# Rows and columns of a DRAM array change places: a stage of its own against element-wise DMAs inside the scans

## The chip, the cores and the metric

The kernel runs as one program on one core of a Trainium2 chip. The metric is device time in microseconds of one execution; the time of the kernel before is the median of 3 runs.

## What is computed

The input is one image of 256 x 256 positions with 128 channels. Two layers work on it, each on a group-normalized copy, and each adds its result to the image. The first is row-wise attention with a bias that comes from the pairs. The second is a selective scan over the image in four directions, and the change lies in it:

```python
x_flat = xc.reshape(b, d, L)                                    # rows, one after the other
x_t    = jnp.transpose(xc, (0, 1, 3, 2)).reshape(b, d, L)       # columns, one after the other
xs     = concat([x_flat, x_t, flip(x_flat), flip(x_t)], axis=1) # k = 0, 1, 2, 3
x_dbl  = einsum('bkdl,kcd->bkcl', xs, x_proj_w)
dts, Bs, Cs = split(x_dbl, [8, 24], axis=2)                     # rate input, B, C
delta  = softplus(einsum('bkrl,kdr->bkdl', dts, dt_w) + dt_b)
h      = exp(delta_t * A) * h + (delta_t * x_t) * B_t           # 65536 steps, 16 states, 256 channels
y      = einsum('bkdn,bkn->bkd', h, C_t)
```

Scans 0 and 2 read the image in row order (2 from the end), scans 1 and 3 in column order (3 from the end). The four results are summed in image order, normalized, gated and projected.

## The kernel before

All data is f32. `build` runs the stages one after the other: `group_stats`, `pair_norm`, `attention`, `conv`, `swap`, `scans`, `output`. What passes between them lies in DRAM (`SCRATCH`): among it `xk`, the scans' input by token, `bk`, B of the four scans, `y`, the sum so far, and the rate input and C of the scans, 24 rows (8 and 16) of 65536 tokens for each scan. `conv` works on 8 image rows at a time and ends each with stores that ACT issues: `mid_dc<-dc` twice (lines 579 and 580), `mid_xk<-xk` (577), `mid_y<-y` (578) and four `mid_bk<-bk` (582). `dc0` has the 48 rows of scans 0 and 2, `dc1` those of scans 1 and 3. Both have their tokens in row order.

Scans 1 and 3 want their 48 rows in column order. `swap` (lines 585 to 612) makes that array, `dcT`, from `dc1`. In two halves, it loads 96 partitions of 128 x 128 elements into the tile `a` (16 DMAs of SP, pieces of 512 bytes), copies them with the two axes exchanged into `o` on ACT and DVE by turns (lines 606 and 608), and stores them (32 DMAs of ACT, line 610).

`scans` takes the scans in the order k = 0, 2, 1, 3. Each has 64 blocks of 1024 tokens. In each scan the first 4 and the last 6 blocks are written out, and the 54 between run in a hardware loop of 3 passes with 18 blocks each, whose DRAM addresses come from registers. The order of the instructions on every engine is written by hand (`tc.manual_schedule()`), in 32 steps a block, one for each state m and half h of the channels:

- `recur`: DVE runs the recurrence along the 1024 tokens (`hs`, line 858, TENSOR_TENSOR_SCAN); after the second half POOL multiplies `hs` with C, which `fetch` brought (`cc<-mid_dc` or `cc<-mid_dcT`, line 826, one row of C broadcast to 128 partitions, ring of 4).
- `turn`: PE brings the input term of the next step to PSUM (`mm`, lines 846 and 848), in rings of two.
- `collect`: PE turns `hs` three states back and sums it over the states (line 617).
- `decay`: ACT computes `da` = exp(delta A) (line 839) four steps ahead, in a ring of six.
- `scale`: ACT scales with B (`dg` and `but`, lines 833 and 835) six steps ahead.
- `advance` runs the preparation of the next block as a list of pieces, each due at a step. The ones that matter here are `size` in steps 6 and 8 (`e<-mm`, line 759, ACT, after PE's `rate`, line 750), `exp` in step 9, `log` in step 10, and `one_plus` and `rest` in steps 11 and 12.

SP issues all loads and stores of the scans: `dt` (line 724, step 21 of the block two before), `bt` and `xk` (step 0 of the block before), `yb` (step 16), the store of `y` (step 8 of the block after) and a `cc` for every second step. ACT issues none in the scans. Every DMA takes one of eight completion semaphores by turns and waits until the last DMA on that semaphore has ended. The recording layer also makes a DMA wait for an earlier one that writes the same array, if it can't see that the places are distinct.

Of the kernel before, what the change touches and what calls it, by code (L numbers as in the profile page):

```python
# [28 lines left out]
F32 = mybir.dt.float32  # L29
# [6 lines left out]
P = 128  # L36
N = 256
# [7 lines left out]
KD = 4  # L45
RC = DR + DS
# [16 lines left out]
def load_consts(tc, pool, io):  # L63
    nc = tc.nc
    c = Consts()
    c.ident = pool.tile([P, P], F32, name="ident")
    nc.sync.dma_start(out=c.ident, in_=io["c_ident"])
    c.group = pool.tile([P, P], F32, name="group")
    nc.sync.dma_start(out=c.group, in_=io["c_group"])
    c.eps = pool.tile([P, 1], F32, name="eps")  # L70
    nc.vector.memset(c.eps, EPS)
    c.gn1 = pool.tile([P, 2], F32, name="gn1")
    c.gn2 = pool.tile([P, 2], F32, name="gn2")
    return c
# [507 lines left out]
                nc.scalar.dma_start(out=io["bk"][k, toks, :].rearrange("(j p) n -> p j n", p=P), in_=bk[:, k])  # L582


def swap(tc, io, src, dst):

    nc = tc.nc
    B = 128
    Q = 16
    PR = KD // 2 * RC  # L590
    s = io[src].rearrange("p (i h w) -> i p h w", h=B, w=N)
    d = io[dst].rearrange("p (w i h) -> i p w h", i=N // B, h=B)
    with tc.tile_pool(name=f"s_{dst}", bufs=1) as sb:
        for j in range(N // B):
            a = sb.tile([P, B, B], F32, name="a")
            for i in range(N // B):
                for q in range(0, B, B // 4):
                    nc.sync.dma_start(
                        out=a[i * PR : (i + 1) * PR, q : q + B // 4, :],
                        in_=s[i, :, q : q + B // 4, j * B : (j + 1) * B],  # L600
                    )
            o = sb.tile([P, B, B], F32, name="o")
            for n, q in enumerate(range(0, B, Q)):
                to, of = o[0 : N // B * PR, q : q + Q, :], a[0 : N // B * PR, :, q : q + Q].rearrange("p h w -> p w h")
                if n % 2:
                    nc.scalar.copy(to, of)
                else:
                    nc.vector.tensor_copy(to, of)
                for i in range(N // B):
                    nc.scalar.dma_start(  # L610
                        out=d[i, :, j * B + q : j * B + q + Q, :], in_=o[i * PR : (i + 1) * PR, q : q + Q, :]
                    )


def turned(nc, c, out, in_, start, stop):

    nc.tensor.matmul(out, in_, c.ident, is_transpose=True, start=start, stop=stop, skip_group_check=True)  # L617


def scans(tc, io, c):  # L620
# [11 lines left out]
    nc = tc.nc  # L632
    TB = 1024
# [6 lines left out]
    with tc.tile_pool(name="e_w", bufs=1) as wp, tc.tile_pool(name="e_1", bufs=1) as sb1, tc.tile_pool(  # L640
        name="e_2", bufs=2
# [43 lines left out]
        class Block:  # L685
# [44 lines left out]
            def advance(self, now, after):  # L730
                if self.pieces is None:
                    self.pieces = begin(self)
                while self.pieces and self.pieces[0][:2] <= (now, after):
                    _, _, f, *args = self.pieces.pop(0)
                    f(*args)

        def begin(B):

# [86 lines left out]
        def fetch(B, m):  # L825
            nc.sync.dma_start(out=ccs[m % 4], in_=B.S.C[m : m + 1, B.where()].partition_broadcast(P))
# [26 lines left out]
        def recur(B, m, h):  # L853
            hs = hss[(B.n * DS + m) % HS]
            o, d0, d1 = hs[:, h, :], das[((B.n * DS + m) * NH + h) % DA], d1s.pop(0)
            if B.S.back:
                o, d0, d1 = o[:, ::-1], d0[:, ::-1], d1[:, ::-1]
            nc.vector.tensor_tensor_scan(o, d0, d1, state[:, m, h : h + 1], ALU.mult, ALU.add)  # L858
            if h == NH - 1:

                last = 0 if B.S.back else TB - 1
                last = hs[:, :, last : last + 1]
                nc.vector.tensor_reduce(state[:, m, :], last, AX.X, ALU.max)  # L863
                for x in range(NH):
                    nc.gpsimd.tensor_tensor(hs[:, x, :], hs[:, x, :], ccs[m % 4], ALU.mult)  # L865
# [16 lines left out]
        def collect_some(most):  # L882

            for x in list(waiting):
                if most == 0:
                    break
                B, _, _, j = x
                if B.slot(j) // PB in B.free:
                    waiting.remove(x)
                    collect(*x)  # L890
                    most -= 1

        def evict(B, after, part):

            n = NJ // PB // 2
            for g in range(part * n, (part + 1) * n):
                to = B.y[:, g * PB : (g + 1) * PB, :]
                nc.vector.tensor_tensor(to, to, pys[g], ALU.add)
                if after:
                    after.free.add(g)  # L900
            if part == 1:
                nc.sync.dma_start(out=B.rows(io["y"]), in_=B.as_rows(B.y))
# [5 lines left out]
        def body(blocks, before, after):  # L908

            own = len(blocks)  # L910
            at_hand = dict(enumerate(blocks + after))
            if before:
                at_hand[-1] = before
                before.free = before.started = set(range(NJ // PB))
                d1s[:] = [mms[count[0] % 2]]

            def at(u):
                x, s = divmod(u, U)
                return (at_hand[x], *divmod(s, NH)) if x in at_hand else None

            def do(f, u):
                if at(u):
                    f(*at(u))

            if before is None:
                blocks[0].load()
                blocks[0].load_tokens()
                blocks[0].advance(U, True)
                blocks[0].free = set(range(NJ // PB))
                blocks[1].load()  # L930
                for m in range(4):
                    fetch(blocks[0], m)
                for u in range(3 * NH):
                    do(scale, u)
                for u in range(4):
                    do(decay, u)
                do(turn, 0)
            for x, B in enumerate(blocks):
                nxt = at_hand.get(x + 1)
                for s in range(U):  # L940
                    u = x * U + s
                    m, h = divmod(s, NH)
                    if s == 0 and nxt:
                        nxt.load_tokens()
                    if s == 21 and x + 2 in at_hand:
                        at_hand[x + 2].load()
                    if s == 16:
                        nc.sync.dma_start(out=B.as_rows(B.y), in_=B.rows(io["y"]))
                    if nxt:
                        nxt.advance(s, False)  # L950
                    recur(B, m, h)
                    do(turn, u + 1)
                    if at(u - LAG * NH):
                        waiting.extend((*at(u - LAG * NH), j) for j in range(NJ))
                    collect_some(len(waiting) if s == LAG * NH - 1 else share.get(s, 10))
                    if x - 1 in at_hand and s in (6, 8):
                        evict(at_hand[x - 1], B, (s - 6) // 2)
                    if nxt:
                        nxt.advance(s, True)
                    do(decay, u + 4)  # L960
                    if u == 0:
                        nc.scalar.preload_act_table_set("natural_log_exp_and_others")
                    do(scale, u + 3 * NH)
                    if h == NH - 1 and at(u + 1 + 3 * NH):
                        fetch(*at(u + 1 + 3 * NH)[:2])
            if not after:
                waiting.extend((*at(u), j) for u in range(own * U - LAG * NH, own * U) for j in range(NJ))
                collect_some(len(waiting))
                for part in range(2):
                    evict(blocks[-1], None, part)  # L970
            assert not waiting


        n = NT // TB
# [103 lines left out]
@with_exitstack  # L1078
def build(ctx: ExitStack, tc: tile.TileContext, io):
    const = ctx.enter_context(tc.tile_pool(name="const", bufs=1))  # L1080
    c = load_consts(tc, const, io)
    group_stats(tc, io, c)
    pair_norm(tc, io, c)
    attention(tc, io, c)
    conv(tc, io, c)
    swap(tc, io, "dc1", "dcT")
    scans(tc, io, c)
    output(tc, io, c)

# [44 lines left out]
```

## Time and profile before

| what | value |
|---|---|
| median of 3 runs | 28440.62 us (28439.84 to 28441.89) |
| profiled execution, span | 28447.5 us |
| PE busy | 26610.1 us (94%) |
| ACT busy | 25332.4 us (89%) |
| DVE busy | 24922.2 us (88%) |
| POOL busy | 22944.4 us (81%) |
| DMA packets | 1923996, 3630.07 MB |
| queue q1 (issued by SP) | 1424722 packets, 3339.77 MB, 34.6% of 16 engines |
| queue q10 (issued by ACT) | 496640 packets, 255.88 MB, 3.2% of 16 engines |
| DVE hs L858 | 8192 instructions, 2340 ns each |
| POOL hs L865 | 8192 instructions, 2380 ns each |
| ACT da L839 | 8192 instructions, 1139 ns each |
| ACT o L606 and DVE o L608 in swap | 8 each, median 3642 and 1906 ns |
| ACTq L610, stores of swap | 32, median 1231 ns to issue, from 4626.5 us to 4731.9 us |

The profiled execution has no time of its own beside its span; the span is 6.9 us longer than the median of the runs. In the profile, `ACTq` and `SPq` are instructions of ACT's and SP's sequencers, here the issues of DMAs, which are not counted as busy time. `L` and a number is a line of the kernel. "ACT e L759 <- PE mm L750" is a wait of ACT at line 759 that PE's line 750 ended.

### The profile page before, as it was taken

Reading aid. Unit: us, or ns where it says so; the run is one execution under the profiler, and the core shown is the slowest. Engines: PE = TensorE matmul, PEld = TensorE weight load, DVE = VectorE, ACT = ScalarE, POOL = GpSimd, SP = SyncE. Lnnn points to the kernel's source line nnn. Section 1 sums busy time; section 2 is a strip of 40 time slices with the busy share of each in tenths; the row PEclk is TensorE's granted clock in tenths of the full one; section 3 lists DMA queues with packets and bytes.
Section 4 is the critical chain, followed back from the end, with each engine's and each line's share of the span. In section 5 each row is a group of like instructions: output and inputs, shape, how many; then the busy total and the mean of one; then the engine's idle time right before and its main releaser. Section 6 shows DMA issues by size and latency. Waiting matters only on the chain. (4 is left out here: it accounts for less than half of the span.)

```text
span 28447.5 us, 528099 instructions
## 1 busy us (share of the span) xinstructions
PE 26610.1 (94%) x196490; PEld 22529.2 (79%) x196490; DVE 24922.2 (88%) x24253; ACT 25332.4 (89%) x49673; POOL 22944.4 (81%) x10118
## 2 busy tenths in 40 slices
PE   8999996999999999999999999999999999999998
PEld 3555444888888888888888888888888888888884
DVE  4777665999999999999999999999999999999987
ACT  6875224999999999999999999999999999999987
POOL 2443002999999999999999999999999999999983
PEclk9999998999999999999999999999999999999999
DMA  5112345433433333333334333333333333333335
GB/s 206 55 50 71 111 116 115 132 132 129 133 130 133 132 131 132 132 131 132 128 132 133 131 133 132 131 132 129 132 132 130 133 132 129 132 130 132 133 132 172
DMA packets 1923996, 3630.07 MB, mean 128 GB/s; under 512 B 532297, under 2 KB 1240009, under 8 KB 1889490
## 3 DMA queue, kind: packets, MB, share of 16 engines
q1 hardware_dynamic: 1424722, 3339.77, 34.6%
q10 hardware_dynamic: 496640, 255.88, 3.2%
q8 instruction: 1568, 25.69, 0.4%
q14 instruction: 1066, 8.73, 0.1%
HBM read 3002.42 MB, written 592.84 MB: 126 GB/s over the span
## 5 line engine op out<-in xcount | busy, mean ns | idle before, releaser
L865 POOL TENSOR_TENSOR hs<-hs,cc 128x1024 f32<-128x1024 f32 x8192 | 19202.5, 2380 | 1346.1 <-DVE state L863 679.9
L858 DVE TENSOR_TENSOR_SCAN hs<-da,state,mm 128x1024 f32<-128x1024 f32 x8192 | 18976.6, 2340 | 1465.4 <-PE mm L848 1074.7
L846 PE MATMUL mm<-dg,dxt 128*128 128x128 f32 x65536 | 9305.0, 287 | 1065.1 <-DVE hs L858 886.1
L846 PEld LDWEIGHTS mm<-dg,dxt 128*128 128x128 f32 x65536 | 8328.4, 199 | 2257.9 <-DVE hs L858 1897.8
L839 ACT ACTIVATE da<-delta,A 128x1024 f32<-128x1024 f32 x8192 | 9328.4, 1139 | 112.2 <-PEq L984 76.0
L617 PE MATMUL y<-ident,hs 128*128 128x128 f32 x65536 | 8511.4, 275 | 1.4 <-POOL hs L865 1.4
L835 ACT ACTIVATE but<-dxt,bt 128x256 f32<-128x256 f32 x16384 | 8150.2, 497 | 11.4 <-DVE dxt L794 11.4
L617 PEld LDWEIGHTS y<-ident,hs 128*128 128x128 f32 x65536 | 7494.1, 143 | 1.9 <-POOL hs L865 1.9
L833 ACT ACTIVATE dg<-ident,bt 128x128 f32<-128x128 f32 x16384 | 6393.1, 390 | 0.2
L848 PE MATMUL mm<-ident,but 128*128 128x128 f32 x32768 | 5092.5, 280 | 0.0
L848 PEld LDWEIGHTS mm<-ident,but 128*128 128x128 f32 x32768 | 4011.4, 146 | 0.0
L750 PE MATMUL mm<-dt,dtw 9*128 9x512 f32 x4096 | 2033.0, 615 | 265.9 <-DMA bt<-mid_bk 184.5
L385 POOL TENSOR_TENSOR an<-ex,rs 128x1024 f32<-128x1024 f32 x512 | 970.2, 1895 | 1024.5 <-PE tp L394 566.3
L780 POOL TENSOR_TENSOR lw<-lw,e 128x1024 f32<-128x1024 f32 x512 | 1207.7, 2384 | 336.3 <-ACT lw L766 336.3
L750 PEld LDWEIGHTS mm<-dt,dtw 9*128 9x128 f32 x4096 | 680.7, 184 | 959.5 <-issue 733.3
L500 POOL MEMSET pad<- 128x10 f32 x32 | 3.7, 117 | 1650.0 <-PE ps L537 1639.9
L777 POOL TENSOR_TENSOR lw<-lw,w 128x1024 f32<-128x1024 f32 x512 | 1202.9, 2375 | 0.0
L537 PE MATMUL ps<-pad,w 128*128 128x512 f32 x2048 | 954.8, 610 | 161.0 <-ACT xi L525 161.0
L372 ACT ACTIVATE ex<-sc,nm 128x256 f32<-128x256 f32 x2048 | 1013.7, 499 | 0.4
L759 ACT ACTIVATE e<-mm 128x1024 f32<-128x1024 f32 x512 | 524.7, 1025 | 522.1 <-PE mm L750 521.9
L355 DVE CUSTOM_DVE_ANT_0 sc<-ps,bias 128x256 f32<-128x256 f32 x2048 | 746.2, 421 | 117.3 <-PE ps L340 117.3
L394 PEld LDWEIGHTS tp<-ident,an 128*128 128x128 f32 x4096 | 467.5, 141 | 470.7 <-POOL an L385 235.1
(137 smaller groups left out, 18522.4 us busy)
## 6 DMA issues: line engine op xcount, KB each, us to landing
cc<-mid_dc SPq DMA_DIRECT2D x2048, 512.0 KB
cc<-mid_dcT SPq DMA_DIRECT2D x2048, 512.0 KB
xk<-mid_xk SPq DMA_DIRECT2D x256, 1024.0 KB
yb<-mid_y SPq DMA_DIRECT2D x256, 1024.0 KB
mid_y<-yb SPq DMA_DIRECT2D x256, 1024.0 KB
xt<-mid_xT SPq DMA_DIRECT2D x64, 1024.0 KB
mid_xk<-xk ACTq DMA_DIRECT2D x32, 2048.0 KB
mid_y<-y ACTq DMA_DIRECT2D x32, 2048.0 KB
```

Of the source, the lines that this page charges most:

```text
L372: nc.scalar.activation(exs[u][:, x, :], scs[u][:, e, jt, :], AF.Exp, scale=-1.0, bias=nms[u][:, e, jt : jt + 1], accum_out=sms[u][:, x : x ...
L617: nc.tensor.matmul(out, in_, c.ident, is_transpose=True, start=start, stop=stop, skip_group_check=True)
L750: nc.tensor.matmul(pu[:, q : q + T], dtw[0 : DR + 1, k, h * P : (h + 1) * P], B.dt[0 : DR + 1, q : q + T], start=True, stop=True,)
L777: nc.gpsimd.tensor_tensor(B.lw[:, h, :], B.lw[:, h, :], B.w[:, h, :], ALU.add)
L780: nc.gpsimd.tensor_tensor(B.lw[:, h, :], B.lw[:, h, :], B.e[:, h, :], ALU.add)
L833: nc.scalar.activation(dg[:, j, :], c.ident, AF.Copy, scale=B.bt[:, B.slot(j), m : m + 1])
L835: nc.scalar.activation(bu[:, j, :], B.dxt[:, DJ + j, :], AF.Copy, scale=B.bt[:, at, m : m + 1])
L839: nc.scalar.activation(da, B.delta[:, h, :], AF.Exp, scale=A[:, B.S.k * NH + h, m : m + 1])
L846: nc.tensor.matmul(d1[:, j * P : (j + 1) * P], B.dxt[:, j, hc], dg[:, j, :], start=True, stop=True)
L848: nc.tensor.transpose(d1[:, j * P : (j + 1) * P], bu[:, j - DJ, hc], c.ident)
L858: nc.vector.tensor_tensor_scan(o, d0, d1, state[:, m, h : h + 1], ALU.mult, ALU.add)
L865: nc.gpsimd.tensor_tensor(hs[:, x, :], hs[:, x, :], ccs[m % 4], ALU.mult)
```

## The change

The function `swap(tc, io, src, dst)` and its call go. In `scans` a nested function of the same name takes its place: for a block B of scan 0 (B.S.x = 0) or 2 (B.S.x = 1) it takes 24 rows of `dc1`, those of scan 1 or 3, and moves four image columns of them to where they lie in column order in `dcT`. There is one DMA for each column, issued by ACT, from DRAM to DRAM: it reads 24 x 256 elements that lie 1 KB apart, and writes them as 24 runs of 256 neighbours. Over the 64 blocks of the two scans all 256 columns of all 48 rows are moved. It is issued in step 10, after `exp` and `decay` and `scale` of step 9, and before `log`.

```diff
-def swap(tc, io, src, dst):
-    nc = tc.nc
-    B = 128
-    Q = 16
-    PR = KD // 2 * RC
-    s = io[src].rearrange("p (i h w) -> i p h w", h=B, w=N)
-    d = io[dst].rearrange("p (w i h) -> i p w h", i=N // B, h=B)
-    with tc.tile_pool(name=f"s_{dst}", bufs=1) as sb:
-        for j in range(N // B):
-            a = sb.tile([P, B, B], F32, name="a")
-            ...
@@ in scans
+        def swap(B):
+            G = KD // 2
+            rows = slice(B.S.x * RC * KD // 2 // G, (B.S.x + 1) * RC * KD // 2 // G)
+            W = TB // N
+            of = io["dc1"][rows].rearrange("p (h w) -> p h w", w=N)[:, :, B.where(N)]
+            to = io["dcT"][rows, B.where()].rearrange("p (w h) -> p w h", h=N)
+            with nc.allow_non_contiguous_dma(reason="rows and columns change places"):
+                for w in range(W):
+                    nc.scalar.dma_start(out=to[:, w, :].unsqueeze(2), in_=of[:, :, w : w + 1])
@@ in body, for each step s of a block
                     if s == 0 and nxt:
                         nxt.load_tokens()
+                    if s == 10 and not B.S.across:
+                        swap(B)
                     if s == 21 and x + 2 in at_hand:
                         at_hand[x + 2].load()
@@ in build
     conv(tc, io, c)
-    swap(tc, io, "dc1", "dcT")
     scans(tc, io, c)
```

More of the change, by code (lines that the diff above doesn't have):

```diff
@@ L582, in conv @@
                 nc.scalar.dma_start(out=io["bk"][k, toks, :].rearrange("(j p) n -> p j n", p=P), in_=bk[:, k])
-def swap(tc, io, src, dst):
-    nc = tc.nc
-    B = 128
-    Q = 16
-    PR = KD // 2 * RC
-    s = io[src].rearrange("p (i h w) -> i p h w", h=B, w=N)
-    d = io[dst].rearrange("p (w i h) -> i p w h", i=N // B, h=B)
-    with tc.tile_pool(name=f"s_{dst}", bufs=1) as sb:
-        for j in range(N // B):
-            a = sb.tile([P, B, B], F32, name="a")
[L596 to L612, printed above, removed]
 def turned(nc, c, out, in_, start, stop):
```

## The prediction

> **What bounds it now.** I read the page first (shares of the engines, their course over the span), then one scan block, the waits in the scans, and the timeline of the stage that goes.
>
> ```profile
> PE 26610.1 (94%) x196490; PEld 22529.2 (79%) x196490; DVE 24922.2 (88%) x24253; ACT 25332.4 (89%) x49673; POOL 22944.4 (81%) x10118
> ...
> ACT  6875224999999999999999999999999999999987
> ```
>
> PE leads the totals, but they mix stages. From the eighth slice on, the scans, ACT is full. The cc loads of the first two scans run from 4755.7 to 16208.7 us: 11,453 us for 128 blocks, 89.5 us each. A stretch of about one block (columns: length; busy PE, PEld, DVE, ACT, POOL; granted clock, DMA share, GB/s):
>
> ```profile
> 10000.00:10089.00 89.00, 85.70 (x675) 78.49 (x673) 82.79 (x57) 86.99 (x167) 84.01 (x37) 0.96 0.40 132
> ```
>
> ACT has the most work, 87.0 us, and in the waits from 10000 to 12000 us (22 blocks) it waits in one place only, 40.3 us in all, about 2 us a block, before the step e:
>
> ```profile
> PEld mm L846 <- DVE hs L858: 168.0, 156, 1.6
> ...
> ACT e L759 <- PE mm L750: 40.3, 43, 2.4
> ```
>
> So ACT's order of instructions sets the length of a block. Whatever holds ACT for more than 2 us a block is paid in full, since ACT can't make it up.
>
> **What is removed.** In SP's timeline the stage reaches from its first load to the first load of the scans:
>
> ```profile
> 4578.09 113.12 SPq L598 DMA_DIRECT2D a<-mid_dc  x16
> 4737.14 0.30 SPq L644 DMA_DIRECT2D dtw<-in_dt_wT  x1
> ```
>
> Nothing else is at work meanwhile, and what comes next (dt, bt and xk of scan 0) needs only what conv wrote. The whole 159 us goes.
>
> **What is added.** In each of the 128 blocks of scans 0 and 2 ACT issues four DMAs, between exp and log of step 10. Each has 24 x 256 = 6,144 elements of 4 bytes, none next to its neighbour in the source, so 6,144 descriptors (24,576 a block, 3.1 million in all; the profile counts 1.9 million packets now). None uses SBUF, and SP's queue issues nothing of it.
>
> *Engines.* In the trace's DMA records the dtw load of 8 rows ends in 8 four-byte completion writes, transfers of 48 and 128 rows in 16. A transfer of 24 rows does not divide by 16; I take 12, the largest divisor below it: 512 descriptors an engine. (Bound: 16 engines, 384 each.)
>
> *Time of a descriptor.* The trace has no element-wise transfer from DRAM to DRAM. The nearest rows, as windows:
>
> ```profile
> 2595.05:2596.05 1.00, 1.00 (x4) 0.49 (x3) 0.59 (x1) 0.73 (x2) 0.00 (x0) 1.00 0.86 6
> 4573.00:4576.00 3.00, 0.00 (x0) 0.00 (x0) 0.00 (x0) 0.00 (x0) 0.00 (x0) 0.50 0.82 86
> 4578.00:4737.00 159.00, 0.00 (x0) 0.00 (x0) 14.68 (x8) 29.23 (x8) 0.00 (x0) 0.50 1.01 158
> ```
>
> The first is the load of cw, 4-byte reads from DRAM: 1,663 records in 1 us over 16 engines, 9.6 ns per descriptor and engine. The second is the end of conv's bk stores, 64-byte writes to DRAM: 11.8 ns. The third has the loads of a, 512 bytes read at a pitch of 1 KB: at worst 433 in 2 us, 74 ns, with the data itself in it and only 48 partitions to write. I take 11.8 ns, the row that writes small pieces to DRAM. If an engine read and wrote in turn it would be 9.6 + 11.8 = 21.4 ns; upper end 74 ns. A rule speaks against the change: the Trainium skill, "DMA: Bandwidth & Descriptors", section "Specifications", says that transfers under 512 bytes are done as read-modify-write. The 64-byte row shows no price of that; no row has a 4-byte write to DRAM. If the rule bites there, the sum is that of the second rival below.
>
> *Does ACT go on after issuing?* Its timeline at the end of conv says no:
>
> ```profile
> 4557.93 0.40 ACTq L577 DMA_DIRECT2D mid_xk<-xk  x1
> 4559.19 1.50 ACTq L578 DMA_DIRECT2D mid_y<-y  x1
> 4560.73 14.45 ACTq L582 DMA_DIRECT2D mid_bk<-bk  x4
> ```
>
> The first 2,048 descriptors are accepted in 0.40 us, later ones only as earlier ones drain: when the fourth bk issue ends, 12,288 have been issued and 9,166 started, 3,122 still waiting, about 200 an engine. ACT stands meanwhile; "ACT xi L525" waits 549.1 us in 31 blocks for it, 17.7 us each. The same page's section "Issuing engines are not separate DMA queues" calls the sequencer's time to start a DMA usually small relative to the DMA; this row has it at the size of the DMA, and by the rule the sum would be that of the first rival below.
>
> *Waits.* In the built program the 54 blocks of each scan's loop, whose addresses are in registers, have every swap DMA wait for the completion of the one before. The 10 blocks outside the loop have no such wait. ACT's own queue stands behind it: log, the next da, dg and but, for which PE's turn and DVE's scan wait, and POOL's product after them. da is 4 units ahead and a unit is 89.5 / 32 = 2.8 us, so the others run on some 11 us and then stand as well.
>
> *Sum for one block.* From issue to first packet 0.86 us (L610, 4702.72 to 4703.58), from last packet to the waiter 0.80 us (4736.65 to 4737.45, DVE's memset of dt), data 512 x 11.8 ns = 6.04 us: 7.7 us for a waited DMA. In the loop: three of them, 23.1 us, and of the fourth 0.86 + 312 x 11.8 ns = 4.5 us until its last 200 fit: 27.6 us. Outside it: 0.86 + (2,048 - 200) x 11.8 ns = 22.7 us. In the first 11 us two cc fetches share the engines, 8 packets each of 159 ns: 2.5 us. The 2 us that ACT waits for e now I don't credit: in the stretch without PE work above the granted clock was 0.50, and PE at half speed after each stall will hold up e and turn about as long. That is 30.1 and 25.2 us.
>
> 108 x 30.1 = 3,251 and 20 x 25.2 = 504, together 3,755; less 159 is +3,596 us. The profiled span is 28,447.5 us, 6.9 above the median, and the page shows no time outside it, so the difference goes on the median: 28,440.6 + 3,596 = 32,040 us.
>
> Ends: 16 engines, 9.6 ns, no cc, 2 us credited: 3 x 5.35 + 0.86 + 184 x 9.6 ns = 18.7 us in the loop, 13.7 outside; 108 x 16.7 + 20 x 11.7 - 159 = +1,875, 30,320 us. 21.4 ns: 48.1 and 42.9 us, +5,870, 34,310 us. 74 ns: 3 x 39.5 + 24 + 2.5 = 145 and 140 us, +18,300, 46,700 us.
>
> Beside this: the 16 DMA engines have 0.40 of 89 us = 36 us of work a block; 12 get 24 us more, within a block of 119 us, so they are no bound. SP's DMAs share completion semaphores with the new ones; a cc fetch is issued 6 units, 17 us, ahead, and POOL stands through the stall, so I put it at nothing; uncovered, it would cost a landing of about 2 us a block, +0.26 ms.
>
> **Rivals.**
> 1. *Hidden, faster.* ACT's issues return at once as those of xk did (0.40 us), and the chain of waits is met in the 2 us of slack; then only the stage goes: 28,440.6 - 159 = 28,280 us. It decides where ACT is held below 159 / 128 + 2 = 3.2 us a block. For it: DMA share 0.40, the result is needed a scan later. Against it: bk's issues, with a quarter as many descriptors an engine, and the waits. One waited transfer alone is past 3.2 us.
> 2. *Slow elements.* 4-byte writes into the same piece of DRAM, or reads at a pitch of 1 KB, go at over 21.4 ns. At 36 ns: (0.86 + 18.4 + 0.80) x 3 + 0.86 + 11.2 + 2.5 = 74.9 and 69.9 us, +9,320, 37,760 us; at 74 ns 46,700 us. For it: the slow loads of a, and no row with such a write. Against it: those loads also moved 128 times the bytes.
> 3. *The exchange moves, but ACT isn't held in the loop beyond the ring* (waits met early): 22.7 us everywhere, 128 x 22.7 - 159 = +2,750, 31,190 us; inside my band.
>
> **How the numbers follow.** Forecast with rival 3 inside (9.6 to 21.4 ns; 30,320 to 34,310 us) 0.72; rival 2 0.23; rival 1 0.04; no measurable difference, where both would cancel, 0.01. The range takes in the band and rival 2 up to 36 ns: 30,320 to 37,760 us; beyond lie about 0.15 above and 0.05 below. Faster than 0.2% (57 us, about what a measurement of this kernel can tell) 0.04, same 0.01, slower 0.95.
>
> **What would show it.** Right: no stage between conv and scans; four swap DMA issues a block on ACT, the first three each some 8 us apart in the loop, the fourth's row about 4 us long; blocks of scans 0 and 2 near 119 us, of 1 and 3 still 89.5; q10 with 3.1 million 4-byte packets more; DVE waiting for da once a block. Wrong: blocks of 89 us, issues of under 1 us with log following at once, a swap transfer far from 6 us, or cc fetches as the longest wait.

## The result: twice the time

The changed kernel takes 57,527 us (median of 4 runs, 57,387 to 57,614), against 28,441 us. The ratio is 2.022, with a 95% interval of 2.019 to 2.025. The direction was forecast; the size was not: 29,086 us were added where 3,600 were predicted, and the time lies far above the range (37,760 us). Of the spread of cases, it is rival 2, slow elements, and beyond its dearest figure (46,700 us).

The page of the changed kernel, the lines that answer to those of before (the last is from its part 3):

```profile
PE 27689.3 (48%) x196490; PEld 23421.5 (41%) x196490; DVE 24997.0 (43%) x24245; ACT 25401.4 (44%) x49665; POOL 22879.0 (40%) x10118
...
ACT  7623232222222222332222222222223699999998
...
DMA  3147875666788888888878887666588633333334
...
q10 hardware_dynamic: 3623424, 255.90, 32.7%
```

The engines do the same work as before in twice the span. In the first two scans, now slices 4 to 31 of 40, ACT is busy in two or three tenths, while the DMA engines go up to eight tenths. The last two scans look as before. ACT's queue q10 has 3.13 million packets more, as counted, and moves no more bytes than before.

The stage is gone, as predicted. SP's first load of the scans starts 157.5 us earlier (4579.63 instead of 4737.14 us):

```profile
4579.63 0.31 SPq L614 DMA_DIRECT2D dtw<-in_dt_wT  x1
```

The ACT timeline of one block of the loop shows where the time goes. The first row is the first swap DMA, the second the other three, the third the `log` behind them (last column: the idle time before it, and who ended it):

```profile
9927.23 0.81 ACTq L715 DMA_DIRECT2D mid_dcT<-mid_dc  x1
10008.80 126.42 ACTq L715 DMA_DIRECT2D mid_dcT<-mid_dc  x3
10135.32 1.91 ACT L746 ACTIVATE lw<-e 128x2048 f32<-128x2048 f32 x1 [201.79 <-DMA mid_dcT<-mid_dc]
```

The second DMA goes out 81.6 us after the first, and all four take until 10,135 us to be issued. The prediction had some 8 us for each. ACT stands for 201.8 us where 27.6 were worked out. In the window from 10008.80 to 10135.20 us no engine is busy and the DMA moves less than 1 GB/s at a share of 0.63 (columns as in the prediction):

```profile
10008.80:10135.20 126.40, 0.00 (x0) 0.00 (x0) 0.00 (x0) 0.00 (x0) 0.00 (x0) 0.50 0.63 0
10000.00:10317.00 317.00, 92.48 (x672) 83.68 (x672) 83.41 (x56) 87.43 (x166) 83.69 (x36) 0.64 0.70 35
```

The second line is about one block: the same 87 us of ACT, now in 317 instead of 89 us. The groups of the page that stand for the loss, first of the changed kernel, then the two of them that the page before has, too (there is no wait before `log` there):

```profile
L845 POOL TENSOR_TENSOR hs<-hs,cc 128x1024 f32<-128x1024 f32 x8192 | 19135.9, 2371 | 6622.0 <-DMA cc<-mid_dc 5213.2
...
L746 ACT ACTIVATE lw<-e 128x2048 f32<-128x2048 f32 x256 | 487.9, 1906 | 24926.3 <-DMA mid_dcT<-mid_dc 19758.5
...
L819 ACT ACTIVATE da<-delta,A 128x1024 f32<-128x1024 f32 x8192 | 9330.3, 1139 | 2971.6 <-DVE hs L838 2777.1
```

```profile
L865 POOL TENSOR_TENSOR hs<-hs,cc 128x1024 f32<-128x1024 f32 x8192 | 19202.5, 2380 | 1346.1 <-DVE state L863 679.9
...
L839 ACT ACTIVATE da<-delta,A 128x1024 f32<-128x1024 f32 x8192 | 9328.4, 1139 | 112.2 <-PEq L984 76.0
```

ACT's idle time before `log` is 24,926 us, 194.7 us for each of the 128 blocks. With what ACT waits more than before at da (2,859), e (413), dg (638) and but (312), about 29,150 us come together; less the stage of 158 us, that is the 29,092 us between the two spans to within about 100. The second part, 4,220 us, is ACT waiting for the others. The first line points to its source: POOL now waits 5,213 us for cc, for which it hardly waited before. So the slow transfers hold ACT first, and the loads on the same DMA engines come late as well. By the DMA records the 4 KB packets of q1 take 640 ns on average in the first two scans, instead of 192; the median is 159 ns in both, so it is a part of them that waits long. That such transfers delay the others even when ACT doesn't stand is tried below, with one DMA a block.

### The profile page after: what moved, and what is told of

It is laid out like the page before. It is cut to its first block, busy times and chain, and to the rows that moved or that the text cites. A ratio compares the mean times of both kernels' runs of the same rounds, so it can differ in the third digit from the quotient of the medians.

```text
span 57539.0 us, 531089 instructions
## 1 busy us (share of the span) xinstructions
PE 27689.3 (48%) x196490; PEld 23421.5 (41%) x196490; DVE 24997.0 (43%) x24245; ACT 25401.4 (44%) x49665; POOL 22879.0 (40%) x10118
## 5 line engine op out<-in xcount | busy, mean ns | idle before, releaser
L826 PE MATMUL mm<-dg,dxt 128*128 128x128 f32 x65536 | 9775.5, 295 | 26097.8 <-DVE hs L838 25143.2
L826 PEld LDWEIGHTS mm<-dg,dxt 128*128 128x128 f32 x65536 | 8725.3, 206 | 27250.3 <-issue 25005.6
L746 ACT ACTIVATE lw<-e 128x2048 f32<-128x2048 f32 x256 | 487.9, 1906 | 24926.3 <-DMA mid_dcT<-mid_dc 19758.5
L587 PE MATMUL y<-ident,hs 128*128 128x128 f32 x65536 | 8907.7, 282 | 2545.8 <-POOL hs L845 1787.8
L587 PEld LDWEIGHTS y<-ident,hs 128*128 128x128 f32 x65536 | 7785.3, 147 | 2581.9 <-POOL hs L845 1847.0
L828 PE MATMUL mm<-ident,but 128*128 128x128 f32 x32768 | 5278.1, 287 | 310.8 <-issue 294.4
L828 PEld LDWEIGHTS mm<-ident,but 128*128 128x128 f32 x32768 | 4174.6, 150 | 488.5 <-issue 471.7
L774 DVE TENSOR_TENSOR dxt<-mm,xk 128x1024 f32<-128x1024 f32 x512 | 615.7, 1202 | 604.7 <-PE mm L770 560.5
```

The lines of the kernel that those rows point to most:

```text
L826: nc.tensor.matmul(d1[:, j * P : (j + 1) * P], B.dxt[:, j, hc], dg[:, j, :], start=True, stop=True)
L828: nc.tensor.transpose(d1[:, j * P : (j + 1) * P], bu[:, j - DJ, hc], c.ident)
```

## The experiments

Two questions were open: which side of the element-wise transfer is slow, the reads at a pitch of 1 KB (theory R) or the writes of 4 bytes (theory W); and how much of the loss is ACT standing, how much contention. Each diff shows the lines that matter, the rest is left out.

**Reads alone.** The four transfers end in SBUF, already in column order; a store of whole rows follows a block later.

```diff
-nc.scalar.dma_start(out=to[:, w, :].unsqueeze(2), in_=of[:, :, w : w + 1])
+nc.scalar.dma_start(out=sw[:, w, :].unsqueeze(2), in_=of[:, :, w : w + 1])   # sw: SBUF, 24 x (4 x 256)
+nc.scalar.dma_start(out=to, in_=sw)                                          # a block later, runs of 4 KB
```

> The same 4-byte reads from DRAM at a pitch of 1 KB, four DMAs of ACT in step 10, but into an SBUF tile of 24 partitions that is already in column order; one DMA of ACT writes it to DRAM a block later, in runs of 4 KB. The result is complete. Theory W (4-byte writes to DRAM, 16 of them next to each other in one piece of 64 bytes, are what takes 117 ns each): the element loads go at some 10 to 12 ns per descriptor and engine, 5 to 6 us a DMA; ACT stands about 15 to 20 us a block; 30,200 to 31,000 us. Theory R (4-byte reads at a pitch of 1 KB are what is slow): each load still takes some 60 us, ACT still stands about 160 us a block, 50,000 us or more.

30,341 us. In the list for the tile sw, the element loads, and the wait for them:

```profile
L718 ACTq DMA_DIRECT2D sw<-mid_dc x512: 815/5392/11633, 4649.9 to 18055.4; - x171
...
  ACT lw L753: 2098.1, 128
```

An issue has a median of 5.4 us (columns: least, median, most, in ns). By the DMA records the 24,576 elements of a block start within 26 us (median), 13 ns for each of 12 engines, with the loads of the scans beside them. The reads are not it.

**Writes alone.** One load of 16-byte runs into SBUF, and a block later the four element-wise stores from there.

```diff
+nc.scalar.dma_start(out=sw.rearrange("p (h w) -> p h w", h=N), in_=of)
-nc.scalar.dma_start(out=to[:, w, :].unsqueeze(2), in_=of[:, :, w : w + 1])
+nc.scalar.dma_start(out=to[:, w, :].unsqueeze(2), in_=sw[:, w, :].unsqueeze(2))
```

> The other half: one DMA of ACT loads 24 x 256 runs of 16 bytes (four columns) at a pitch of 1 KB into SBUF, and a block later four DMAs of ACT write element-wise from SBUF to DRAM, 4 bytes each, neighbours next to each other, as the changed kernel does. The result is complete. Theory W: the four stores take some 60 us each, ACT stands 150 to 200 us a block, 50,000 us or more; the load of 16-byte runs takes 6 us. Theory R: the load takes some 60 us, but alone and without ACT waiting for it at once; the stores take 6 us each; 30,000 to 32,000 us.

57,640 us, the time of the changed kernel again. The list for sw:

```profile
L716 ACTq DMA_DIRECT2D sw<-mid_dc x128: 1428/44472/52742, 4649.9 to 45141.2; - x128
...
  ACT lw L755: 29373.3, 128
```

The issues of the stores follow each other by 78.0, 58.1 and 58.3 us (medians), as in the changed kernel (81.0, 60.8, 60.0), though they now read SBUF. The load, issued last, is held 44 us; it stands in the queue behind the fourth store, which still has to drain. Theory W holds, and it takes no DRAM on the source side.

**Writes 1 KB apart.** The kernel before with its stage, and four DMAs a block that copy columns to the same place in a scratch array, so that no write has its neighbour next to it.

```diff
+to = io["dcX"][rows].rearrange("p (h w) -> p h w", w=N)[:, :, B.where(N)]
+nc.scalar.dma_start(out=to[:, :, w : w + 1], in_=of[:, :, w : w + 1])        # step 10, w = 0..3
```

> The kernel before, its swap stage included, and beside it four element-wise DMAs from DRAM to DRAM of ACT in step 10 as in the changed kernel, but into a scratch array in the source's own order: every 4-byte write lies 1 KB from the one before it instead of next to it. Nothing reads the scratch. Theory W1 (it is the neighbours: 16 writes that follow each other into the same 64 bytes of DRAM wait for each other): some 10 to 15 ns per descriptor and engine, 5 to 8 us a DMA, ACT held 20 to 30 us a block, 31,000 to 32,500 us. Theory W2 (any 4-byte write to DRAM costs about 117 ns an engine, wherever it lies): 60 us a DMA, 55,000 us or more.

32,752 us, 4,310 more than the kernel before beside it, 33.7 us a block. The list for the scratch array, and the wait for it:

```profile
L743 ACTq DMA_DIRECT2D mid_dcX<-mid_dc x512: 521/532/18190, 4808.3 to 20458.0; - x171
  ACT lw L774: 3825.0, 109
```

The first issue is followed by the others after 17.5, 11.3 and 11.3 us, where the changed kernel has 81.0, 60.8 and 60.0. Less the 1.7 us of latency that the prediction used, 11.3 us would be 19 ns per descriptor, a sixth of the 115 of neighbours (60.4 us). The DMA records tell the writes from the wait for their completion. From the first to the last start, the 6,144 writes take 6.9 us here, 14 ns for each of an engine's 512, as expected; in the changed kernel they take 49.3 us, 96 ns (medians of the third transfer in the loop). The last completion comes 2.6 us after the last recorded write here, and 9.4 us after it there. It is the neighbours.

**Larger neighbours.** Three DMAs a block into scratch, neighbouring pieces of 16, 32 and 64 bytes.

```diff
+of = io["dc1"][rows].rearrange("p (h w) -> p h w", w=N)[:, 0 : TB // e, 0:e]
+to = io[f"dcX{e}"][rows, B.where()].rearrange("p (h w) -> p h w", w=e)      # e = 4, 8, 16 elements
+nc.scalar.dma_start(out=to, in_=of)                                         # steps 10, 28, 30
```

> The kernel before, its swap stage included, and three DMAs of ACT a block from DRAM to DRAM into scratch arrays that nothing reads: 98 KB each, read at a pitch of 1 KB and written as neighbouring pieces of 16 bytes (6,144 descriptors, step 10), 32 bytes (3,072, step 28) and 64 bytes (1,536, step 30). Each is short or is left alone for at least half a block, and the trace's DMA records give the rate by size. Theory W1 (neighbouring writes into the same 64 bytes wait for each other): slow as 4 bytes are for 16 and 32 bytes, about 100 ns and more per descriptor and engine, and about 12 ns for 64. Theory W2 in the form that a write below some size is dear: the same for 16, then a step at 32 or 64. If all three run at 8 to 15 ns, the dear case is 4 bytes alone. Time 28,440 plus about 2.4 us of issuing less 2 us of slack a block, to 28,700 us, if ACT is held only by its issues; with a 16-byte DMA of 60 us still not more than 29,500 us.

29,301 us. By the DMA records the 6,144 pieces of 16 bytes take 52.0 us (median of the blocks), 102 ns for each of an engine's 512; the 3,072 of 32 bytes take 3.8 us, 15 ns; the 1,536 of 64 bytes 3.1 us, 24 ns. So 16 bytes are as slow as 4, and at 32 bytes it is over. W1 had expected 32 bytes to be slow still; that part of it falls.

**Single elements, apart by 16, 32 and 64 bytes.** Against the run before, each piece is cut down to its first element.

```diff
-to = io[f"dcX{e}"][rows, B.where()].rearrange("p (h w) -> p h w", w=e)
+to = io[f"dcX{e}"][rows, B.where()].rearrange("p (h w) -> p h w", w=e)[:, :, 0:1]   # and of[..., 0:1]
```

> The kernel before, its swap stage included, and three element-wise DMAs of ACT a block from DRAM to DRAM into scratch arrays that nothing reads. All write single elements of 4 bytes; what differs is how far apart: 16 bytes (6,144 descriptors, step 4), 32 bytes (3,072, step 16), 64 bytes (1,536, step 26). Theory S (what is slow is a part of a 32-byte piece of DRAM written while an earlier write into the same piece is still on its way): the first takes some 50 us, 100 ns per descriptor and engine, as the 16-byte pieces did; the second and the third run at 15 to 25 ns, 4 to 7 us and 3 us. Theory N (small writes that lie near each other, in the same page or channel of the DRAM, hinder each other, in the same piece or not): the second and the third are slow too, 100 ns per descriptor and engine, 26 and 13 us. Time 29,000 to 29,500 us by S, since the first alone is much like the 16-byte one of before; over 30,000 us by N.

30,053 us, which is the range of theory N. But the first DMA, 16 bytes apart, was not done when the second was issued 12 steps later, in 124 of 128 blocks (its last completion comes 59 us after its issue, median), and the second ran into its tail: nothing follows for 32 bytes. The third took 1.9 us, against theory N. The run was repeated without the first:

> As the run before, without the writes 16 bytes apart, whose tail lay over the DMA behind it: single 4-byte elements written 32 bytes apart (3,072 descriptors, 256 an engine, step 4), 64 bytes apart (1,536, 128 an engine, step 16) and 128 bytes apart (768, 64 an engine, step 26). Theory S (only writes into the same 32-byte piece hinder each other): all at 10 to 25 ns, 3 to 6 us, 2 to 3 us and 1 to 2 us; under 28,600 us. Theory S2 (the piece has 64 bytes): the first is slow, 12 to 26 us, the others as by S. Theory N (small writes near each other hinder each other in general): all near 50 to 100 ns, 13 to 26, 6 to 13 and 3 to 6 us.

28,484 us. Writes 32 bytes apart take 18.7 us, 73 ns per descriptor; 64 bytes apart 1.9 us, 15 ns; 128 bytes apart 0.76 us, 12 ns. That is theory S2. Together with the pieces: a write of 4 or 16 bytes is slow when the one before it goes into the same 64 bytes, and 32 bytes at a time are not, though two of them share 64.

All rows of the table are from the DMA records (medians): the time from the first to the last start of a transfer, divided by the descriptors of one of its 12 engines.

| write to DRAM | next one after | ns per descriptor and engine |
|---|---|---|
| 4 bytes (changed kernel) | 4 bytes | 96 |
| 16 bytes | 16 bytes | 102 |
| 4 bytes | 32 bytes | 73 |
| 32 bytes | 32 bytes | 15 |
| 64 bytes | 64 bytes | 24 |
| 4 bytes | 64 bytes | 15 |
| 4 bytes | 128 bytes | 12 |
| 4 bytes | 1 KB | 14 |
| 4 bytes read at 1 KB, written to SBUF (spread version below) | - | 8 |

**ACT or contention.** One of the four DMAs a block, beside the kernel before.

```diff
+nc.scalar.dma_start(out=to[:, 0, :].unsqueeze(2), in_=of[:, :, 0:1])          # to: scratch, as the change writes it
```

> The kernel before, its swap stage included, and one of the changed kernel's four DMAs a block into a scratch array (three columns in four are left out). ACT's issue should return in 0.8 us, and the 60 to 80 us of the transfer run beside the scans. If what costs the changed kernel its time is that ACT stands while the next DMA waits for the one before, this kernel takes 28,440 to 29,500 us. If the slow writes hold up cc on the 16 DMA engines for as long as they last, POOL waits for cc in most of the block and it is 31,000 us or more.

34,044 us, 43.8 us a block, though ACT is held by its issue for a median of 0.81 us only. The transfer takes 90 us by the DMA records. Who waits is told by the waits from 10000 to 12000 us, here and in the kernel before:

```profile
POOL hs L872 <- DMA cc<-mid_dc: 626.2, 41, 48.0
ACT da L846 <- DVE hs L865: 355.2, 80, 41.8
```

```profile
POOL hs L865 <- DVE state L863: 71.0, 37, 3.3
```

In the kernel before, POOL's longest wait in that window is for DVE's state, 71 us. So the slow writes cost even a kernel that never waits for them: the loads of cc run on the same engines and come late (4 KB packets of q1 take 422 ns on average here), and ACT waits for DVE, which waits for what POOL and PE still hold. The reading that only ACT's standing counts falls.

**A version that keeps the exchange beside the scans.** Element-wise reads into SBUF, which the first experiment showed to be cheap, issued by SP and spread over the block.

```diff
+if s == 2 and x - 1 in at_hand and not at_hand[x - 1].S.across:
+    store(at_hand[x - 1])                    # nc.sync: dcT <- sw, 24 runs of 4 KB
+if s in (3, 10, 17, 24) and not B.S.across:
+    swap(B, (s - 3) // 7)                    # nc.sync: sw[:, w] <- one column of dc1, 6,144 elements
```

> As the run with element-wise reads into SBUF, but issued by SP and spread: one column in each of steps 3, 10, 17 and 24, the store of 4 KB runs by SP in step 2 of the next block. ACT issues nothing. Theory W: each load takes 5 to 6 us on the DMA engines, within the 17 us by which cc is fetched ahead; only the stage goes: 28,280 us, up to 28,500 if cc is late now and then. Theory R: SP's queue and the DMA engines carry four loads of 60 us a block of 89 us, cc comes late: over 45,000 us.

> Element-wise reads into SBUF, issued by SP in steps 3, 10, 17 and 24 and stored in runs of 4 KB a block later, once more and timed against the kernel before. It took 28,298 us in one look. Expected 28,280 to 28,310 us, a ratio of 0.9945 to 0.9955: the stage of 159 us is gone and up to 20 us come back as contention.

28,298 us in the first run; timed, 28,288 us (28,286 to 28,298, 5 runs) against 28,441, a ratio of 0.9947 (0.9933 to 0.9960). It beats both kernels. 153 of the 159 us of the stage are saved. SP's issues take 0.83 us each, nobody waits for sw, and nearly all elements of a transfer (6,050 of 6,144) start within 4.1 us (median). A block looks as before, with the DMA share at 0.59 instead of 0.40:

```profile
L717 SPq DMA_DIRECT2D sw<-mid_dc x512: 777/831/1170, 4636.5 to 16059.3; - x171
```

```profile
10000.00:10089.00 89.00, 84.51 (x675) 76.98 (x673) 83.04 (x58) 87.36 (x169) 84.07 (x37) 0.98 0.59 134
```

**Runs of 16 bytes, exchanged by DVE.** A quarter of the descriptors, and one copy a block.

```diff
+nc.sync.dma_start(out=sw.rearrange("p (h w) -> p h w", h=N), in_=of)                      # step 3
+nc.vector.tensor_copy(so.rearrange("p (w h) -> p w h", h=N), sw.rearrange("p (h w) -> p w h", h=N))   # step 28
+nc.sync.dma_start(out=to, in_=so)                                                         # step 2, next block
```

> Runs of 16 bytes (four columns) instead of single elements: one DMA of SP in step 3 loads 24 x 256 runs into SBUF, DVE exchanges rows and columns in step 28 (24 x 1024, about 1.1 us), SP stores 4 KB runs in step 2 of the next block. Theory W: the load takes 6 us; DVE has 82.8 us of work in a block of 89, so little of its 1.1 us shows: 28,280 to 28,430 us. Theory R: the load takes 60 us on SP's queue, cc is late by some 40 us a block, about 33,500 us.

28,688 us, slower than before by 250 and than expected. The load is as fast as expected (some 9 ns: 6,050 of the 6,144 pieces start within 4.3 us, median). The copy is not:

```profile
L721 DVE COPY so<-sw x128: 1142/1281/6979, 4699.8 to 16453.1; 24x1024 f32<-24x1024 f32 x128
```

35 of the 128 copies take over 4 us, with a median of 6.4, the others 1.2. The blocks lose 3.2 us on average against the spread version's nothing. Which copies take five times as long can be seen in the trace. Each of the 35 begins with 0.4 to 1.4 us left of a multiply of POOL, lasts through that one and the two behind it, and ends 0.9 us after the third. Each of the 93 short ones begins with at most 0.3 us left, and POOL's next multiply takes 3.2 us (median) instead of 2.4. It looks as if a copy of DVE and a multiply of POOL took turns here; that is read from the order in the trace, and no run tests it.

## Why the prediction was wrong

- **What bounds it, what goes.** Right. ACT sets the block, and the stage's 159 us went (157.5 by the first load of the scans).
- **Time of a descriptor: the step that failed.** "I take 11.8 ns, the row that writes small pieces to DRAM." A transfer measured 60.4 us instead of 7.7. Less the latencies of the sum, that is 115 ns per descriptor, almost ten times the term and above its upper end of 74. By the DMA records 96 ns are the writes themselves, and the rest lies behind the last write: the completion came 9.4 us after it where the sum had 0.80. The row taken wrote 64 bytes, whole; the changed kernel writes 4, sixteen in a row into the same 64 bytes, and in the runs' table those two lie on the two sides of a cliff. The prediction said that no row had such a write and that the rule of the Trainium skill ("DMA: Bandwidth & Descriptors", section "Specifications", under 512 bytes a read-modify-write) might bite there; it then went by the row. The runs show a price on small writes, but not on all under 512 bytes: 32-byte neighbours run at 15 ns, and so do 4 bytes that lie 64 apart. An end of the range that comes from loads of 512 bytes was no bound on it. (Two readings and a sum beside it are slightly off, without weight for the result: the window of cw holds 1,553 records and not 1,663, the loads of a go down to 388 in 2 us, and the block at 21.4 ns adds up to 47.9 us and not 48.1.)
- **Engines and counts.** 6,144 descriptors a DMA: right, 3.13 million packets more. 12 engines: right as well, if the four-byte completion writes are counted as the prediction counted them. In the run with larger neighbours q10 has 10,752 four-byte records instead of 6,144, 12 more for each of its 384 new DMAs.
- **ACT does not go on.** Right in kind; two sizes were off, both small beside the main term. A first issue of 512 an engine returned in 0.8 us, so the queue takes more than the 200 an engine read from conv, and the fourth DMA costs ACT 0.8 us, not 4.5. In the loop the three waits came as predicted: from the first issue to the end of the fourth, a block has 206 us (median), against 149 to 183 in the blocks outside it, where the second issue stood for 62 us (median) instead.
- **The same structure with the right term.** 3 x 60.4 + 0.8 = 182 us a block in the loop; some 20 us more come from the first transfer (82.2 us in the loop), which runs beside the loads of the block, as the single one did that took 90 us. The writes 1 KB apart test the structure at a speed near the predicted one: 33.7 us a block there at 14 ns, 30.1 predicted for 11.8 ns.
- **"They are no bound", the DMA engines, and cc "at nothing".** Wrong at this speed: POOL's waits for cc are 5,213 us. The margin of 17 us by which cc is issued ahead is nothing against transfers of 60 us on the same engines.
- **Rival 1** asked for holds under 3.2 us. The spread version is that rival made true, by other means, and it came to 28,288 us where the rival said 28,280.

## What to carry to other kernels

An element-wise DMA has two sides, and they cost differently: let its scattered side be the read, into SBUF, and write to DRAM in whole runs. When a term decides the sum and no row of the profile shows that very access, measure it by itself or give its range the width of ignorance, since the nearest row can lie on the other side of a cliff. And a slow transfer is not hidden because nobody waits for it: look who shares its DMA engines.

## What the runs showed of the hardware

- Writes to DRAM of 4 or 16 bytes take 73 to 102 ns per descriptor and engine when the next one goes into the same 64 bytes. With 32 or 64 bytes at a time, or 64 bytes and more from one to the next, it is 12 to 24 ns.
- Such a transfer starts fast and then crawls. In the block above some 2,100 of the 6,144 descriptors start in the first 8 us, and the last hundreds take tens of us. By the steps of the completion semaphore, which the trace shows going up once for each engine that ends, the 12 engines of the second and third transfers in the loop end between 34 and 61 us after the issue (medians), the last of them 9 to 10 us after the last recorded write. Why they end so far apart stays open, and so does whether it is the DRAM or the DMA engine that waits.
- Element-wise reads of DRAM at a pitch of 1 KB cost 8 ns per descriptor and engine (13 ns with four transfers in a row), and a DMA of 512 descriptors an engine is issued in 0.8 us into an idle queue.
